# Reordering one period of attention A, a double-buffered last attention B and compact keys in a two-attention, two-feed-forward kernel

## The chip, the cores and the metric

The kernel runs on one core of a Trainium2 chip. The metric is the device time of one execution in microseconds (us). Engines are named as in the profile: PE (TensorE), with PEld for its weight loads, DVE (VectorE), ACT (ScalarE), POOL (GpSimd) and SP (SyncE, here only a queue that issues DMAs).

## The reference

Input x has 8 batches of 512 tokens with 256 features; all is float32. Four residual layers follow each other, each behind a layer norm:

```python
x = x + attn_a(norm(x))
x = x + ffn(norm(x))
x = x + attn_b(norm(x))
x = x + ffn(norm(x))
```

```python
# attn_a: 16 heads of 64; per token and head, a 64 x 64 causal table of q_i * k_j
scores = einsum('bshq,bshk->bshqk', Q / 8, K), masked above the diagonal
attn = einsum('bshqk,bshk->bshq', softmax(scores), V) @ Wo + bo
# attn_b: usual causal attention over 512 tokens, 16 heads of 16
y = softmax(q @ k.T / 4, causal) @ v;  y @ W_proj + b_proj
# ffn: hidden 1024, ternary weights with a scale per row
h = silu(x @ w1) * (x @ w2);  h = gelu(h @ h1);  h = gelu(h @ h2);  h @ w3
```

Attention A is unusual: no token looks at another. Each token and head has a table of products q_i * k_j, its exponential, and two sums over j, with weights 1 and v_j. It is element-wise work for DVE, POOL and ACT, not for PE.

## The kernel before

**Two streams.** The first stream is attention A (class AttentionA). Its unit is a *period*: one batch b, one of NG = 4 groups of 4 heads and one of NT = 4 tiles of 128 tokens, 128 periods in all. The second stream (after_a) is the rest: feed-forward 1, attention B and feed-forward 2 of each batch. It runs one batch behind A and shares the engines with it. The last batch's second stream has no attention A beside it.

**Order.** The kernel is recorded with a manual schedule: instructions stand on each engine in the order in which the Python calls them, and each engine works in that order. `step(n)` writes one of four steps of a period, in three parts, so a period has twelve *slots*. After each part the second stream is drawn on, generator by generator, until the cost it has announced with `yield` has reached its share of `total` = 301.7 per 16 periods. Small steps of the second stream (scales, layer norm, copies, products of hi and low halves) are put off with `later` and called at the next `flush`.

**A period.** The causal table of 64 x 64 is cut into squares off the diagonal. There are four units: u = 0 and 2 are the 32-squares of two heads each (tile `w`, 128 x 4096, three buffers), u = 1 the 16-squares of four heads (`w16`, one buffer), u = 3 the squares of 8, 4, 2 and 1 (`ws`). For a unit:

- `scores` (L796): products q * k, on POOL for u = 0 and 2 and on DVE for 1 and 3. For u = 0 also the diagonal, `acc` (L783).
- `exps` (L810, with L805 for the diagonal): exponential on ACT.
- `weigh` (L820, L817): times v on DVE.
- `halve` (L826): a DMA issued from POOL adds the upper half of the tile to the lower one (not for `ws`).
- `fold` (L831): POOL adds halves once more, for the 32-squares.
- `gather` (L857): DVE reduces what is left to sums per row, `red`.
- `add_rows` (L864): POOL adds the sums into `acc`; `small_squares` (L847, L864) does so for the squares of 2 and 1.

Then `invert` (L868, DVE), `divide` (L872, POOL), `turn_group` (L880, PE transposes), the copy `att` (L730, ACT), `project_out` (L888, L483, PE) and `new_x` (L899, ACT). Ahead of a period stand `project` (L753 for k, L758 for q and v, PE), which also has SP load the next group's weights, and `keep_qk` (L773 and L774, ACT copies of k and q). For the first group of a batch, `normalise`, the transposes `turn_x` (L559) and their copy come earlier still.

**PSUM.** Of eight banks two hold `qv`, five rotate in `ps_f` for the second stream, and one, `bank`, is cut into two halves of 256 columns for k, the transposed x, the transposed result and its projection. `half_bank()` gives the halves in turn.

**Second stream.** `Normed` normalises a tile: `moments` on DVE (L535, L536), `scales` on POOL (L540 to L543), `normed` on ACT (L549, L553), transposes on PE (L559), a copy on ACT (L988), for the feed-forward its low part on DVE (L995). The feed-forward multiplies in two halves, hi and low: gates L1064, `silu` L1040 (ACT), L1043 (DVE), L1047 (ACT) and L1048 (POOL); hidden layers L1126 (PE), L1097 and L1098 (ACT), L1102 (DVE); the last product L1159. Weights are loaded by DMAs issued from POOL (L946). Attention B: projections `pqkb` L1205 with copies L1226, values `pvb` L1243, and for 4 groups of four heads and 4 key blocks `scores` (L1260, mask L1264, exponential L1267) and `values` (L1272).

Of the kernel before, what the change touches and what calls it, by code (L numbers as in the profile page):

```python
# [9 lines left out]
F32 = mybir.dt.float32  # L10
# [25 lines left out]
BG = BH * SLOT // P  # L36

FH = 1024
MC = FH // P
HB = 2048  # L40

# [243 lines left out]
def fast_path(ctx: ExitStack, tc: tile.TileContext, k, t, flag):  # L285
# [154 lines left out]
    wbqk_d = dram.tile([P, HB], F32, name="wbqk_d")  # L440
# [5 lines left out]
    def later_weights():  # L446
# [7 lines left out]
        wbqk = block("wbqk").rearrange("p (c f) -> p c f", c=DC)  # L454
        rows = block("rows")
        wbvp = block("wbvp")[:, : 2 * DC * D].rearrange("p (j c f) -> p j c f", j=2, c=DC)
        n_qk = 2 * BG * P
        nc.sync.dma_start(wbqk, t.w_bqkb.rearrange("(c p) j f -> p c (j f)", p=P))
        nc.sync.dma_start(wbvp[:, 0], t.w_bvb.rearrange("(c p) f -> p c f", p=P))
        nc.sync.dma_start(wbvp[:, 1], t.w_bp.rearrange("(c p) f -> p c f", p=P))  # L460
        nc.sync.dma_start(rows[0:1, :n_qk], t.w_bqk[D - 1 : D].rearrange("o j f -> o (j f)"))
        nc.sync.dma_start(rows[0:1, n_qk : n_qk + D], t.w_bv[D - 1 : D])
        yield
        for w, off, width in ((wbqk, 0, 2 * GW), (wbqk, 2 * GW, 2 * GW), (wbvp[:, 0], 0, D)):
            row = rows[0:1, n_qk if width == D else off :][:, :width]
            pss = [less_row(w[:, c, off : off + width], c, row, 0) for c in range(DC)]
            yield
            for c, ps in enumerate(pss):
                nc.scalar.copy(w[:, c, off : off + width], ps)
            yield  # L470
# [20 lines left out]
    turn = [0]  # L491


    bank = ps_a.tile([P, 2, GW], F32, name="bank")
    halves = [0]

    def half_bank():
        halves[0] ^= 1
        return bank[:, halves[0], :]
# [78 lines left out]
    def pieces(w, n, off, nsq, cols):  # L578

# [7 lines left out]
        if n < 16:  # L590
            e, ev = (
                w[:, a * SMALL + off : a * SMALL + off + nsq * n * n].rearrange("p (x i j) -> p x i j", i=n, j=n)
                for a in range(2)
            )
            yield e, ev, lambda v: of_rows(v).unsqueeze(3), lambda v: of_cols(v).unsqueeze(2)
            return
        both = w.rearrange("p (b a x i j) -> p a b x i j", a=2, x=nsq, i=n, j=JB)
        if n == 32:
# [7 lines left out]
        else:  # L606
            for k in range(n // JB):
# [5 lines left out]
                )  # L613

    class AttentionA:
# [3 lines left out]
        def __init__(self):  # L619
# [5 lines left out]
            self.ready, self.sums = set(), []  # L625
            self.todo = [
                (b, i, g, u) for b in range(NB) for g in range(NG) for i in range(NT) for u in range(NU)
            ]
            self.steps = len(self.todo) + 11
# [16 lines left out]
        def at(self, n):  # L646
            return self.todo[n] if 0 <= n < len(self.todo) else (None,) * 4

        def step(self, n):

            weighed = self.at(n - 2)
            if weighed[0] is not None:
                self.weigh(*weighed)
            unit = self.at(n)
            on_pool = unit[3] in (0, 2)
            if on_pool:
                half = self.scores(*unit)
                next(half)
            if weighed[0] is not None:
                self.halve(*weighed)  # L660
            if on_pool:
                next(half, None)
            b, i, g, u = self.at(n + 40)
            if u == 0 and g == 0 and i == 0 and b > 0:
                self.x[b] = load_x(b)
            b, i, g, u = self.at(n + 10)
            if u == 0 and g == 0 and i == 0 and b > 0:
                self.measure(b)
            b, i, g, u = self.at(n + 8)
            if u == 0 and g == 0:  # L670
                self.live["xn"] = normed(self.x[b][:, i, :], *self.rn[b, i], "a")
            b, i, g, u = self.at(n - 5)
            if u == NU - 1:
                self.invert(b, i, g)
            b, i, g, u = self.at(n - 4)
            if u == 1:
                self.gather(b, i, g, u)
            b, i, g, u = self.at(n + 7)
            if u == 0 and g == 0:
                nc.scalar.copy(self.live[b, i], self.live.pop("ps_ln"))  # L680
            if self.at(n - 1)[0] is not None:
                self.exps(*self.at(n - 1))
            yield
            if unit[0] is not None and not on_pool:
                for _ in self.scores(*unit):
                    pass
            for args in self.sums:
                self.add_rows(*args)
            self.sums = []
            b, i, g, u = self.at(n - 5)  # L690
            if u == NU - 1:
                self.divide(b, i, g)
            b, i, g, u = self.at(n - 2)
            if u == NU - 1:
                self.small_squares(b, i, g)

            b, i, g, u = self.at(n - 4)
            if u == 0:
                self.fold(b, i, g, u)
            b, i, g, u = self.at(n - 3)  # L700
            if u == 2:
                self.fold(b, i, g, u)
            b, i, g, u = self.at(n - 9)
            if u == NU - 1:
                self.new_x(b, i, g)
            b, i, g, u = self.at(n + 2)
            if u == 0:
                self.keep_qk(b, i, g)
            b, i, g, u = self.at(n - 7)
            if u == NU - 1:  # L710
                self.turn_group(b, i, g)
            b, i, g, u = self.at(n - 8)
            if u == NU - 1:
                self.project_out(b, i, g)
            b, i, g, u = self.at(n + 3)
            if u == 0:
                self.project(b, i, g)
            yield
            b, i, g, u = self.at(n - 4)
            if u == 2:  # L720
                self.gather(b, i, g, u)
            b, i, g, u = self.at(n - 5)
            if u == 0:
                self.gather(b, i, g, u)
            b, i, g, u = self.at(n - 3)
            if u == NU - 1:
                self.gather(b, i, g, u)
            b, i, g, u = self.at(n - 7)
            if u == NU - 1:
                nc.scalar.copy(self.live["att"], self.live.pop("pta"))  # L730
            b, i, g, u = self.at(n + 8)
            if u == 0 and g == 0:
                self.live[b, i] = lnp.tile([P, DC, P], F32, tag="xnt_a", name=f"xnta_{b}_{i}", bufs=NT)
                self.live["ps_ln"] = turned_over(self.live.pop("xn"), half_bank().rearrange("p (c s) -> p c s", c=DC))
            yield
# [11 lines left out]
        def project(self, b, i, g):  # L747
# [3 lines left out]
            pk = half_bank()  # L751
# [17 lines left out]
        def keep_qk(self, b, i, g):  # L769
# [3 lines left out]
            nc.scalar.copy(kt[:, 0], pk)  # L773
            nc.scalar.copy(kt[:, 1], qv[:, 0])  # L774
            self.live[b, i, g] = [qv, kt]

        def scores(self, b, i, g, n_u):

            qv, kt = self.live[b, i, g][:2]
            if n_u == 0:  # L780
                acc = ap_.tile([P, 2, GW], F32, tag="acc", name=f"acc_{b}_{i}_{g}", bufs=3)
                self.live[b, i, g].append(acc)
                nc.vector.tensor_tensor(acc[:, 0, :], qv[:, 0], kt[:, 0], ALU.mult)  # L783

            if n_u in (0, 2):
                w = wt.tile([P, 4096], F32, tag="w", name=f"w_{b}_{i}_{g}_{n_u}", bufs=3)
            elif n_u == 1:
                w = wt.tile([P, 4096], F32, tag="w16", name=f"w16_{b}_{i}_{g}")
            else:
# [702 lines left out]
```

## Time and profile before

| what | us |
|---|---|
| median of three executions | 3910.99 (3909.09 to 3912.19) |
| the profiled execution, its own time | 3906.43 |
| span of the profiled execution | 3904.6 |
| PE busy | 2962.9 (76%) |
| DVE busy | 3462.5 (89%) |
| ACT busy | 2459.7 (63%) |
| POOL busy | 3081.7 (79%), without the DMA issues |

The costliest groups of instructions, from the page (line, engine, operation, out<-in, count, busy us and mean ns of one, idle time of the engine before them and its releaser):

```profile
L796 POOL TENSOR_TENSOR w<-k 128x1024 f32<-128x1024 f32 x512 | 1077.1, 2104 | 7.5 <-ACT k L774 6.9
L820 DVE TENSOR_TENSOR w<-w,qv 128x1024 f32<-128x1024 f32 x768 | 898.6, 1211 | 9.9 <-ACT w L810 9.9
L831 POOL TENSOR_TENSOR w<-w 128x1024 f32<-128x1024 f32 x256 | 642.6, 2510 | 45.3 <-DMA w<-w 44.9
L826 POOL DMA_DIRECT2D w<-w x384 | 338.9, 883 | 326.2 <-issue 138.4
```

The span falls into a start, a long stretch in which both streams run (from about 480 to 3580 us, some 450 us for each batch), and the last batch's second stream alone (from about 3580 us). An idle time in these lists counts only if the engine is the one that sets the pace there.

### The profile page before, as it was taken

How to read it: one execution, taken by the hardware profiler on the slowest of the kernel's cores; microseconds unless marked ns; L12 is line 12 of the kernel's file. 1: busy time of each engine (PE TensorE's matmuls, PEld its weight loads, DVE VectorE, ACT ScalarE, POOL GpSimd, SP SyncE). 2: the span in 40 equal slices, each digit the busy share in tenths (PEclk: the TensorE clock that was granted, in tenths of full speed). 3: DMA queues.
4: the chain of work that ended last, by engine and by line, in shares of the span. 5: the costliest groups of instructions: out<-in, count | busy, mean ns of one | idle time of the engine just before them, and what ended most of it. 6: DMA issues, size and time to landing. Idle time of an engine off the chain costs nothing.

```text
span 3904.6 us, 37527 instructions
## 1 busy us (share of the span) xinstructions
PE 2962.9 (76%) x12080; PEld 1981.4 (51%) x12080; DVE 3462.5 (89%) x3906; ACT 2459.7 (63%) x3332; POOL 3081.7 (79%) x3052
## 2 busy tenths in 40 slices
PE   5653487687876977778876878778876878778988
PEld 2331264365634655356643656346653556346747
DVE  7999999998999999999999999999989999997216
ACT  3443476577765876667765877667765777655443
POOL 6888888888788888888888888888888888886211
PEclk6556598888987989888997989879898899879999
DMA  8766677678875877768876778768776678666305
GB/s 225 172 137 141 152 194 164 143 176 202 210 156 128 207 196 184 153 157 215 208 166 130 191 195 203 158 140 217 182 191 144 164 192 220 152 137 200 130 25 187
DMA packets 117306, 668.04 MB, mean 171 GB/s; under 512 B 12774, under 2 KB 30825, under 8 KB 42603
## 3 DMA queue, kind: packets, MB, share of 16 engines
q0 software_dynamic: 80640, 587.24, 65.4%
q1 hardware_dynamic: 36460, 78.31, 5.8%
q8 instruction: 98, 1.61, 0.2%
q14 instruction: 108, 0.88, 0.1%
HBM read 253.94 MB, written 8.91 MB: 67 GB/s over the span
## 4 chain that ended last, share of the span: by engine, by line
DVE 43%; PE 17%; POOL 15%; ACT 9%; DMA 8%; issue 8%; SPq 0%; POOLq 0%; DVEq 0%; ACTq 0%
DVE red L857 16%; DVE w L820 11%; DMA w<-w 8%; PE ph L1126 7%; POOL w L796 4%; DVE ws L796 4%; DVE ws L820 3%; ACT w L810 3%; POOL w L831 3%; POOL acc L864 2%; DVE w L796 2%; PE pw L1064 2%; PE pqkb L1205 2%; DVE acc L868 2%; POOL h L1048 2%
## 5 line engine op out<-in xcount | busy, mean ns | idle before, releaser
L1126 PE MATMUL ph<-h,hidden 128*128 128x512 f32 x4096 | 1047.7, 413 | 71.1 <-POOL h L1048 48.7
L796 POOL TENSOR_TENSOR w<-k 128x1024 f32<-128x1024 f32 x512 | 1077.1, 2104 | 7.5 <-ACT k L774 6.9
L810 ACT ACTIVATE w<-w 128x2048 f32<-128x2048 f32 x384 | 734.2, 1912 | 480.8 <-POOL w L796 380.3
L1126 PEld LDWEIGHTS ph<-h,hidden 128*128 128x128 f32 x4096 | 796.0, 196 | 270.5 <-POOL h L1048 57.8
L820 DVE TENSOR_TENSOR w<-w,qv 128x1024 f32<-128x1024 f32 x768 | 898.6, 1211 | 9.9 <-ACT w L810 9.9
L831 POOL TENSOR_TENSOR w<-w 128x1024 f32<-128x1024 f32 x256 | 642.6, 2510 | 45.3 <-DMA w<-w 44.9
L857 DVE TENSOR_REDUCE red<-w 128x128 f32<-128x1024 f32 (+1 forms) x384 | 601.0, 1565 | 65.9 <-POOL w L831 38.3
L826 POOL DMA_DIRECT2D w<-w x384 | 338.9, 883 | 326.2 <-issue 138.4
L864 POOL TENSOR_TENSOR acc<-acc,red 128x256 f32<-128x256 f32 (+1 forms) x640 | 471.2, 736 | 120.0 <-DVE red L857 99.7
L857 DVE TENSOR_REDUCE red<-ws 128x256 f32<-128x2048 f32 (+1 forms) x256 | 435.3, 1741 | 0.0
L758 PE MATMUL qv<-wqv,xnta 128*128 128x512 f32 x512 | 300.4, 717 | 94.4 <-DVE ws L820 78.9
L810 ACT ACTIVATE ws<-ws 128x1920 f32<-128x1920 f32 x128 | 231.5, 1809 | 143.5 <-DVE ws L796 142.9
L1064 PE MATMUL pw<-xnt,gate 128*128 128x512 f32 (+2 forms) x1152 | 308.4, 429 | 14.1 <-ACT silu L1040 5.3
L796 DVE TENSOR_TENSOR w<-qv,k 128x1024 f32<-128x1024 f32 x256 | 301.1, 1218 | 3.7
L796 DVE TENSOR_TENSOR ws<-qv,k 128x1024 f32<-128x1024 f32 (+3 forms) x512 | 299.4, 645 | 0.0
L820 DVE TENSOR_TENSOR ws<-ws,qv 128x1024 f32<-128x1024 f32 (+3 forms) x512 | 295.6, 638 | 3.5 <-ACT ws L810 3.3
L1064 PEld LDWEIGHTS pw<-xnt,gate 128*128 128x128 f32 x1152 | 239.8, 222 | 70.3 <-ACT silu L1040 8.7
L1267 ACT ACTIVATE eb<-psb 128x256 f32<-128x256 f32 (+3 forms) x512 | 181.9, 443 | 129.0 <-PE psb L1264 128.6
L1102 DVE TENSOR_TENSOR h<-ph,h 128x512 fp32r<-128x512 f32 x256 | 169.0, 682 | 97.1 <-ACT ph L1098 91.2
L880 PE MATMUL bank<-ident,acc 128*128 128x128 f32 x256 | 61.1, 327 | 255.4 <-ACT k L773 253.9
L1097 ACT ACTIVATE h<-ph,s_sb 128x512 fp32r<-128x512 f32 x256 | 176.5, 690 | 108.1 <-PE ph L1126 106.0
L753 PE MATMUL bank<-wk,xnta 128*128 128x256 f32 x512 | 166.5, 456 | 99.8 <-ACT x L899 94.8
(153 smaller groups left out, 5042.2 us busy)
## 6 DMA issues: line engine op xcount, KB each, us to landing
w<-w POOLq DMA_DIRECT2D x384, 1024.0 KB, 7.7
hidden<-in_h POOLq DMA_DIRECT2D x128, 1024.0 KB, 7.7
gate<-in_w12p POOLq DMA_DIRECT2D x32, 1024.0 KB, 9.2
w<-in_w3p POOLq DMA_DIRECT2D x16, 1024.0 KB, 5.3
wqv<-wqv_d SPq DMA_DIRECT2D x31, 512.0 KB, 4.6
wo<-in_wo SPq DMA_DIRECT2D x32, 256.0 KB, 6.0
wbqk<-wbqk_d SPq DMA_DIRECT2D x8, 1024.0 KB, 6.8
w<-in_h SPq DMA_DIRECT2D x8, 1024.0 KB, 6.4
```

Source lines behind the costliest of these rows:

```text
L758: nc.tensor.matmul(qv.rearrange("p j f -> p (j f)"), xnt[:, c, :], wqv[:, c, :], start=(c == 0), stop=(c == DC - 1),)
L796: eng.tensor_tensor(e, rows(q).to_broadcast(shape), columns(kt[:, 0]).to_broadcast(shape), ALU.mult)
L810: nc.scalar.activation(e, e, AF.Exp, scale=C**-0.5)
L820: nc.vector.tensor_tensor(ev, e, columns(qv[:, 1]).to_broadcast(list(e.shape)), ALU.mult)
L826: nc.gpsimd.dma_start(w[:, :2048], w[:, 2048:], accum_op=ALU.add)
L831: nc.gpsimd.tensor_tensor(w[:, :1024], w[:, :1024], w[:, 1024:2048], ALU.add)
L857: nc.vector.tensor_reduce(red, self.columns_of(w, n, off, nsq), AX.X, ALU.add)
L864: nc.gpsimd.tensor_tensor(rows, rows, part.rearrange("p a (x i) -> p a x i", i=n), ALU.add)
L1064: nc.tensor.matmul(pj[:, toks], w[:, m % 4, j, c, :], xs[:, p, c, toks], start=(p == 0 and c == 0), stop=(p == 1 and c == DC - 1),)
L1097: nc.scalar.activation(h(0, m), pj, AF.Gelu, scale=scale)
L1126: nc.tensor.matmul(pss[j], w[:, j, c, :], h_in(p, c), start=(p == 0 and c == 0), stop=(p == 1 and c == MC - 1),)
L1267: nc.scalar.activation(es[h], scs[h], AF.Exp)
```

## The change

**The order of a period** is no longer written in `step`, but in a table G["order"] of (slot, action, arguments). `slot(t)` calls for each entry the action of the period n with t = 12 n + slot; actions of one slot come in the order of the table. A period reaches from slot -120 to slot 40.

| action | slot before | slot after |
|---|---|---|
| normalise, turn_x, its copy | -24, -22, -21 | -25, -22, -20 |
| project, keep_qk | -8, -5 | -6, -2 |
| scores u = 0, 1, 2, 3 | 0, 4, 6, 10 | 0 and 1, 4, 6, 10 |
| exps u = 0, 1, 2, 3 | 3, 6, 9, 12 | 3, 6, 9, 12 |
| weigh u = 0, 1, 2, 3 | 6, 9, 12, 15 | 5, 9, 12, 13 |
| halve u = 0, 1, 2 | 6, 9, 12 | 6, 9, 12 |
| fold u = 0, 2 | 13, 16 | 13, 17 |
| small_squares | 16 | 14 |
| gather u = 1, 0, 3, 2 | 15, 17, 20, 20 | 15, 16, 19, 21 |
| adds u = 1, 0, 3, 2 | 16, 19, 22, 22 | 20, 20, 21, 22 |
| invert, divide | 24, 25 | 24, 25 |
| turn_group, copy att | 31, 32 | 28, 32 |
| project_out, new_x | 34, 37 | 33, 40 |

Within a period DVE then does, from the reciprocal on: first product of the next period, `ws` weighing, `w16` reduce, first `w32` reduce, `w16` products, diagonal and first `w32` weighing, reduces of 8 and 4, `w16` weighing, second `w32` reduce, `ws` products, second `w32` weighing. Before, the first `w32` reduce stood behind the `w16` products, the second ahead of the reduces of 8 and 4, and the first product ahead of the reciprocal. POOL: the sums of `w16` and of the squares of 8 and 4 are now added ahead of the `w16` halving, which in turn stands ahead of the last add; before, the `w16` sums were added between the first fold and the small squares.

**PSUM halves.** `half_bank()` is gone; each use has a fixed half: k and the transposed x take half 0, the transposed result and its projection half 1.

**Pace.** The second stream is drawn on after each slot, with the same delay as before and `total` = 298.1.

**Attention B.** Keys are packed 16 columns a head (2 groups of 128 instead of 4); queries keep 32 columns a head, with zeros beside the 16 of the head, and heads are taken in an order that puts two of one key slot into neighbouring groups. Score matmuls keep their number and size; the key projection has two groups fewer. In the last batch (`alone`) the scores take seven PSUM banks in turn (four of `ps_f`, two of `qv`, and `bank`), the exponentials two blocks in turn, and a step's scores stand ahead of the previous step's values.

Other branches that the table opens (sums by transposes on PE, a split of `w16` with POOL, a gelu remainder on PE) are not taken with these values: `sum` is dve, `p16` is 0, `gelu`, `lo`, `div` and `first` are not set.

```diff
+G = {'sum': ['dve', 'dve'], 'p16': 0, 'rot': 3, 'half': [0, 0, 1, 1, 0, 1],
+ 'order': [[12, 'weigh', 2], [40, 'new_x'], [6, 'scores', 2, 0, 2], [9, 'exps', 2], [12, 'exps', 3],
+           [24, 'invert'], [-25, 'normalise'], [6, 'halve', 0], [32, 'keep_att'], [21, 'adds', 3],
+           [3, 'exps', 0], [33, 'project_out'], [0, 'scores', 0, 0, 2], [1, 'scores', 0, 1, 2],
+           [25, 'divide'], [20, 'add32', 0], [12, 'halve', 2], [-120, 'load'], [22, 'add32', 2],
+           [-20, 'keep_x'], [20, 'adds', 1], [6, 'scores', 2, 1, 2], [-30, 'ahead'], [5, 'weigh', 0],
+           [-22, 'turn_x'], [14, 'small_squares'], [-2, 'keep_qk'], [-6, 'project'], [15, 'gather', 1],
+           [10, 'scores', 3, 0, 1], [17, 'fold', 2], [9, 'weigh', 1], [9, 'halve', 1], [6, 'exps', 1],
+           [16, 'sums32', 0], [4, 'scores', 1, 0, 1], [28, 'turn_group'], [19, 'gather', 3], [13, 'fold', 0],
+           [21, 'sums32', 2], [13, 'weigh', 3]]}
...
-    def half_bank():
-        halves[0] ^= 1
-        return bank[:, halves[0], :]
+    def bank_half(j):
+        return bank[:, j, :]
...
+        def slot(self, t):
+            now = []
+            for lo, hi, order in TABLES:
+                for place, (slot, what, args) in enumerate(order):
+                    n, r = divmod(t - slot, 12)
+                    if r == 0 and lo <= n < hi:
+                        now.append((place / len(order), what, self.todo[n] + args))
+            for _, what, args in sorted(now, key=lambda p: p[0]):
+                getattr(self, what)(*args)
...
-        for j in range(2):
-            pps = [None] * BG
+        for j, groups in enumerate((BG, KG)):
+            pps = [None] * groups
...
+        alone = b == NB - 1
+        exps = [block(f"eb_{b}_{n}").rearrange("p (h q) -> p h q", q=S) for n in range(1 + alone)]
...
+        def score_bank(name):
+            n, taken[0] = taken[0] % 7, taken[0] + 1
+            if not alone or n < 4:
+                return ps_f.tile([P, S], F32, tag="pf", name=name)
+            if n < 6:
+                return ps_qv.tile([P, S], F32, tag="qv", name=name)
+            return bank.rearrange("p j f -> p (j f)")
...
-                    scs[h], qk[1][slots[h], g, keys], qk[0][slots[h], g, j * P :], start=True, stop=False
+                    scs[h], qk[1][slots[h], g // 2, keys], qk[0][slots[h], g, j * P :], start=True, stop=False
...
-                if before is not None:
+                if before is not None and not alone:
                     values(*before)
                 es = scores(g, j)
+                if before is not None and alone:
+                    values(*before)
...
-        for n in range(-10, a.steps):
-            for part, _ in enumerate(a.step(n)):
-                if n >= 3 and part == 2:
-                    next(prep, None)
-                while 3 * spent * each < total * (3 * (n - each - 11) + part + 1):
-                    spent += next(done)
+        for at in a.slots:
+            a.slot(at)
+            if at >= 9 and at % 3 == 2:
+                next(prep, None)
+            while spent * 12 * NT * NG < total * (at + 1 - 12 * NT * NG - 33):
+                spent += next(done)
```

## The prediction

> **What bounds the kernel now.** I read the page first (busy shares, slices, chain), then a table of stretches, then the idle time of VectorE and GpSimd by line inside the long stretch, then two timelines.
>
> ```profile
> DVE  7999999998999999999999999999989999997216
> POOL 6888888888788888888888888888888888886211
> DVE 43%; PE 17%; POOL 15%; ACT 9%; DMA 8%; issue 8%; SPq 0%; POOLq 0%; DVEq 0%; ACTq 0%
> ```
>
> VectorE (DVE) is nearly full for 37 of 40 slices with GpSimd (POOL) close behind, and DVE leads the chain. The last three slices are a tail of another kind. The stretches show both (columns: length, busy PE, PEld, DVE, ACT, POOL, clock, DMA share, GB/s):
>
> ```profile
> 480.00:3580.00 3100.00, 2422.51 (x10181) 1643.63 (x10182) 2903.49 (x3289) 2136.48 (x2871) 2630.51 (x2591) 0.88 0.75 177
> 3580.00:3904.60 324.60, 293.73 (x1405) 213.88 (x1404) 110.69 (x140) 128.85 (x251) 58.86 (x96) 0.96 0.35 124
> 2115.30:2181.60 66.30, 49.34 (x181) 35.65 (x181) 59.71 (x83) 42.28 (x58) 56.38 (x64) 0.80 0.63 145
> 2066.60:2090.36 23.76, 16.22 (x97) 7.40 (x96) 23.73 (x25) 14.77 (x28) 20.71 (x19) 0.79 0.66 133
> ```
>
> A period without feed-forward work (the last line) leaves DVE 0.03 us idle: there a new order gains nothing. Over the long stretch DVE is idle 3100 - 2903.5 = 196.5 us, two gate periods (third line) holding 6.6 of it. In the tail TensorE (PE) is busy 90% and sets the end. What ends DVE's idle time in the long stretch, then the same for two rows of POOL:
>
> ```profile
> L857 DVE TENSOR_REDUCE red<-w 128x256 f32<-128x2048 f32 x329 | 515.3, 1566 | 51.5 <-POOL w L831 31.2 <-DMA w<-w 19.2
> L1043 DVE SCALAR_TENSOR_TENSOR silu<-pw,s_sb,silu 128x512 f32<-128x512 f32 x112 | 82.8, 739 | 51.5 <-ACT silu L1040 51.3
> L995 DVE TENSOR_TENSOR xnt<-ps_ln,xnt 128x256 fp32r<-128x256 f32 x56 | 22.4, 413 | 38.9 <-ACT xnt L988 38.9
> L1102 DVE TENSOR_TENSOR h<-ph,h 128x512 fp32r<-128x512 f32 x216 | 141.8, 681 | 26.0 <-ACT ph L1098 25.8
> L864 POOL TENSOR_TENSOR acc<-acc,red 128x256 f32<-128x256 f32 (+1 forms) x549 | 403.9, 736 | 108.4 <-DVE red L857 90.9
> L880 PE MATMUL bank<-ident,acc 128*128 128x128 f32 x218 | 50.0, 316 | 208.7 <-ACT k L773 207.1 <-POOL w L831 1.4
> ```
>
> Only 51.5 us of DVE's idle time belongs to attention A's own reductions; 116 us are feed-forward steps whose code and pace stay.
>
> **The Trainium skill.** "Perfetto Trace Analysis", Identifying Performance Opportunities: take the most occupied engine, find its gaps, and treat regimes apart; this trace has those two regimes. "DMA: Bandwidth & Descriptors", SWDGE vs HWDGE vs iDMA: accumulating DMAs go through GpSimd only; here the halving DMAs hold POOL 0.88 us each, so moving them moves POOL. "TensorE: Matmul & The Clock Gate", Part 3: four K=32 matmuls side by side reach 3.07x and M=32 columns behave alike. The trace agrees for K=32: 8 score matmuls take 1.07 us to the next row, alone 8 x 0.43 = 3.44 (0.43 is the spacing of the 128x512 pqkb loads), 3.2x.
>
> **The change, part by part.**
>
> (1) The last batch's attention B. One group of heads in the tail, ACT then PE:
>
> ```profile
> 3751.73 2.07 ACT L1267 ACTIVATE eb<-psb 128x512 f32<-128x512 f32 x4 [0.71 <-PE psb L1264]
> 3756.01 1.64 ACT L1267 ACTIVATE eb<-psb 128x384 f32<-128x384 f32 x4 [2.21 <-PE psb L1264]
> 3750.33 1.14 PE L1260 MATMUL psb<-qkb,qkb 32*128 32x512 f32 x8
> 3752.38 2.51 PE L1272 MATMUL pyb<-eb,vb 128*32 128x512 f32 x8 [0.58 <-ACT eb L1267]
> 3763.18 1.14 PE L1260 MATMUL psb<-qkb,qkb 32*128 32x512 f32 x8
> ```
>
> PE and ACT take turns: 3763.18 - 3750.33 = 12.85 us a group. With seven score banks, two exponential blocks and the next scores put ahead of the values, they overlap. ACT needs 2.07 + 1.64 + 1.21 + 0.79 + 0.59 (copy) = 6.3. PE needs scores 1.07 + 0.86 + 0.65 + 0.43 = 3.0, masks 4 x 0.33 = 1.3, and values, seen only while they wait for ACT: at most 6.5 as now, at least 2.8 (the skill's 3.07x on 3.44, times 1280/512 columns). I take 2.8: PE 7.1, ACT 6.3, with hand-over 7.5. Gain 4 x (12.85 - 7.5) = 21; with values at 6.5, 4 x (12.85 - 10.8) = 8.
>
> (2) Compact keys: two projection groups fewer, each 4 x 0.43 = 1.7 us of PE and one ACT copy (0.6). In the tail PE carries the end: -3.4. In the seven other batches PE has room (22% idle): 0. The pace total falls by the same 2 x 1.8, so both streams stay in step: 0. Tail: -24.8 (from -11 to -27).
>
> (3) DVE's order. Counts and durations per period do not change. The w32_0 reduce moves ahead of the two w16 products (2.35 us earlier), the w32_2 reduce ahead of the small-square products, the first product behind the reciprocal. Does the earlier reduce find its data? In the plain period the reciprocal starts at 2066.64, POOL's halving issue at 2067.13, and the fold ends at 2070.34 + 2.64 = 2072.98, that is 5.85 after the issue. In the new order the issue is due just after the reciprocal's start, so the fold ends at about +5.95; the reduce comes at reciprocal 1.66 + product 0.33 + small squares 2.2 + w16 reduce 2.3 = +6.5. Half a microsecond in hand, where 2.3 more were: 0 taken, up to +25 (0.2 us in each period) if POOL is late there.
>
> (4) POOL's order. The add of the w16 sums leaves the place behind the first fold, where POOL stood for DVE's reduce (most of the 90.9 us), and the adds of the 8- and 4-squares go ahead of the w16 halving, where POOL waited 2.74 us in the plain period. DMA landing is 7.7 us, so a halving issued earlier lands earlier. What lies behind the stands is the second fold, half the scores and the halvings: the 51.5 us. Taken: half, -25 (bounds 0 and -51). The silu wait ends on ACT, itself behind POOL's h L1048; less standing on POOL gives a fifth: -10 (0 to -25). The xnt chain runs through POOL's small scale steps: -3 (+10 to -15). h L1102 waits for ACT's own speed: 0 (+-10).
>
> (5) PSUM halves, later key copy. L880 waits 207 us for the key copy of the other half: the wait is between halves, so fixing them removes little; turn_group comes three slots earlier and will wait for the x copy instead. qv L758's 48.7 us go: the projection is two slots later and the last weighing two earlier. PE has room, so 0 (+10 to -10). The projection takes its two weight loads on SP along; they land in 4.6 us and are wanted a period later: 0. keep_qk moves from slot -5 to -2, behind the third exponential. Queued behind it on ACT is the ws exponential; DVE's first product and POOL's next scores wait for it. It ends 1.91 + 0.76 = 2.7 us after the second score half; POOL has 0.7 + 3 x 0.75 + 0.9 + 0.7 = 4.5 of other work there, so 1.8 us remain: 0, but a gelu group on ACT (4.0 us with its table load) between the two takes it.
>
> Sum: tail -24.8, long stretch -38: -63 on the execution's own 3906.4 (span 3904.6 plus 1.8) gives 3843.6; the median shown is 4.6 higher, so 3848.
>
> **Rivals.** The bound of no change is 0.2%, 8 us.
> A, forecast, 0.55: 3848, own range 3815 to 3882.
> B, 0.18: the long stretch keeps its idle time because it belongs to the feed-forward steps; for it the 116 us, against it the 51.5. 3911 - 25 = 3886 (to 3902 with slow values).
> C, 0.12: POOL's stands were the root of most gaps, silu and xnt too; half of 196 goes: 3911 - 25 - 98 = 3788, or 3749 at 70%. For it: POOL at 56.4 busy plus some 6 of issues in the 66.3 us gate stretch.
> D, 0.11: slower. The key copy, behind the third exponential and now also behind project_out in the shared bank, comes late; DVE and POOL both stand. It decides from (25 + 8) / 112 periods = 0.3 us a period; a gelu group ahead of it in half the periods, 2.2 us beyond the 1.8 of slack, one half absorbed, is 112 x 0.5 x 1.1 = 62: 3911 + 62 - 25 = 3948. Against it: k was ready early before (in the plain period it ends at 2078.3, the product starts at 2090.0) and three slots are some 6 us.
> E, 0.04: the layout costs what the tail gains, no measurable change; so too if the layout does nothing and the overlap fails.
>
> Chances: faster 0.85, same 0.04, slower 0.11. Range 3780 to 3908: A, B and part of C, leaving about 2 in 10 outside.
>
> **What would show it.** Right: a group of heads in the tail takes 7 to 8 us; DVE idle before the reduces falls to about 25; POOL's wait on red falls under 40; plain periods stay at 23.7. Wrong: the key copy as releaser of DVE acc or POOL w with several us in total (D); idle before the w32_0 reduce grown (3); silu and xnt waits unchanged and the reduces' too (B).

## The result, and the profile after

| what | us |
|---|---|
| median of the changed kernel | 3867.19 (3857.84 to 3870.38) |
| median of the kernel before, beside it | 3911.59 (3909.09 to 3916.82) |
| ratio | 0.9881, 95% interval 0.9859 to 0.9902 |
| the profiled execution of the changed kernel | 3870.38, span 3868.6 |

Faster by 44 us, or 1.2%; 3848 was forecast, 19 us less, and the range held the time. The profiled execution is the slowest of the four; its span is 36 us shorter than that of the kernel before.

The changed kernel has other line numbers: products L801, weighing L836, halving L843, fold L851, reduces L984, adds L998; `project` L749 for k and L754 for q and v, the key copy L771; `turn_group` L1020, its copy `att` L1024, `new_x` (from here on the x copy) L1045; attention B's `pqkb` L1362 with its copies L1383. A plain period is one without feed-forward work beside it. The changed kernel's page, rows of busy tenths and the chain's shares:

```profile
DVE  7999999999999999999999989999989899898216
POOL 6888888888888888888888888888888878788211
DVE 41%; PE 24%; POOL 15%; ACT 7%; issue 7%; DMA 6%; POOLq 0%; SPq 0%; ACTq 0%; DVEq 0%
```

DVE still leads. Its line now has five 8s, all from the 24th slice on, where before there were two, one of them early: some of the gain is lost again in the later batches. At the last reciprocal of a batch's attention A the changed kernel is ahead by 24 us in the fourth batch and by 11 in the seventh. The table of stretches (length, busy PE, PEld, DVE, ACT, POOL, clock, DMA share, GB/s): the long stretch, then one plain period from reciprocal to reciprocal, then the tail.

```profile
480.00:3560.00 3080.00, 2388.43 (x10085) 1639.06 (x10084) 2874.75 (x3272) 2111.86 (x2834) 2626.16 (x2573) 0.87 0.75 176
...
1125.73:1149.33 23.60, 14.13 (x79) 6.48 (x80) 23.60 (x26) 12.90 (x25) 20.97 (x18) 0.78 0.76 164
3560.00:3868.60 308.60, 285.79 (x1428) 215.54 (x1426) 119.40 (x151) 132.23 (x259) 66.39 (x104) 0.95 0.39 138
```

Over the long stretch DVE is idle 3080 - 2874.75 = 205 us, no less than the 196.5 before. The stretch is nevertheless shorter, because DVE has less to do in it: between the 16th and the last reciprocal its busy time falls from 2954.6 to 2938.6 us, most of it since a period takes some 0.12 us less of DVE (the plain one 23.60 instead of 23.72). From the last reciprocal of attention A to the end there are 292.5 us instead of 315.8; the last reciprocal comes 12.8 us earlier. What ends DVE's idle time in the long stretch (busy and mean; idle and releasers), then the same for POOL, PE and ACT:

```profile
L836 DVE TENSOR_TENSOR w<-w,qv 128x1024 f32<-128x1024 f32 x655 | 767.4, 1213 | 48.0 <-ACT w L824 48.0
L984 DVE TENSOR_REDUCE red<-w 128x256 f32<-128x2048 f32 x327 | 506.5, 1568 | 45.4 <-POOL w L851 33.2 <-DMA w<-w 12.0
L1190 DVE SCALAR_TENSOR_TENSOR silu<-pw,s_sb,silu 128x512 f32<-128x512 f32 x112 | 82.5, 745 | 26.8 <-ACT silu L1187 26.8
L1142 DVE TENSOR_TENSOR xnt<-ps_ln,xnt 128x256 fp32r<-128x256 f32 x52 | 20.7, 420 | 30.5 <-ACT xnt L1135 30.5
```

```profile
L998 POOL TENSOR_TENSOR acc<-acc,red 128x256 f32<-128x256 f32 (+1 forms) x545 | 388.1, 712 | 22.1
L801 POOL TENSOR_TENSOR w<-k 128x1024 f32<-128x1024 f32 x435 | 930.4, 2139 | 87.2 <-ACT k L771 86.7
L1020 PE MATMUL bank<-ident,acc 128*128 128x128 f32 x218 | 59.1, 365 | 341.3 <-ACT x L1045 243.2 <-ACT xnta L728 88.6 <-POOL w L851 4.1
L1024 ACT COPY att<-bank 128x256 f32<-128x256 f32 x109 | 41.1, 377 | 31.8 <-PE bank L749 31.8
```

The reduces wait 45 us (51.5 before), silu 27 (51.5), POOL's adds 22 (108). New are 48 us at DVE's weighing behind ACT's exponential (10 in the whole execution before) and 87 us of POOL's products behind the key copy (7 before). PE's transposes wait 243 us for the x copy; before, they waited 207 us for the key copy instead. The tail on PE, one group of heads from its first scores (L1429, 128x512) to the next group's:

```profile
3729.80 1.14 PE L1429 MATMUL psb<-qkb,qkb 32*128 32x512 f32 x8
...
3733.01 1.35 PE L1441 MATMUL pyb<-eb,vb 128*32 128x512 f32 x8
...
3737.43 0.70 PE L1429 MATMUL psb<-qkb,qkb 32*128 32x512 f32 x2
...
3740.95 1.06 PE L1441 MATMUL pyb<-eb,vb 128*32 128x512 f32 x8 [0.23 <-ACT eb L1436]
...
3745.07 0.69 PE L1429 MATMUL bank<-qkb,qkb 32*128 32x512 f32 x1
```

3745.07 - 3737.43 = 7.64 us a group, and 7.63 for the one before it, instead of 12.85. Eight value matmuls of 512 columns take 2.37, 1.35, 1.06 and 1.34 us in the four groups, where they took 2.42 to 2.51 with waits for ACT.

### The profile page after: what moved, and what is told of

It is laid out like the page before. It is cut to its first block, busy times and chain, and to the rows that moved or that the text cites. A ratio compares the mean times of both kernels' runs of the same rounds, so it can differ in the third digit from the quotient of the medians.

```text
span 3868.6 us, 37899 instructions
## 1 busy us (share of the span) xinstructions
PE 2865.3 (74%) x12016; PEld 1963.0 (51%) x12016; DVE 3440.7 (89%) x3906; ACT 2441.4 (63%) x3310; POOL 3092.5 (80%) x3052
## 4 chain that ended last, share of the span: by engine, by line
DVE 41%; PE 24%; POOL 15%; ACT 7%; issue 7%; DMA 6%; POOLq 0%; SPq 0%; ACTq 0%; DVEq 0%
DVE red L984 13%; DVE w L836 12%; PE ph L1283 11%; DMA w<-w 5%; DVE w L801 4%; POOL w L801 4%; DVE ws L801 4%; DVE ws L836 3%; POOL h L1195 2%; DVE acc L1004 2%; PE pqkb L1362 2%; POOL acc L998 2%; ACT w L824 2%; PE qv L754 2%; PE pot L1316 2%
## 5 line engine op out<-in xcount | busy, mean ns | idle before, releaser
L801 POOL TENSOR_TENSOR w<-k 128x1024 f32<-128x1024 f32 x512 | 1096.1, 2141 | 95.4 <-ACT k L771 94.9
L1283 PE MATMUL ph<-h,hidden 128*128 128x512 f32 x4096 | 1068.3, 419 | 43.2 <-POOL h L1195 35.2
L836 DVE TENSOR_TENSOR w<-w,qv 128x1024 f32<-128x1024 f32 x768 | 899.4, 1212 | 52.1 <-ACT w L824 52.1
L1283 PEld LDWEIGHTS ph<-h,hidden 128*128 128x128 f32 x4096 | 811.3, 200 | 248.3 <-POOL h L1195 45.7
L851 POOL TENSOR_TENSOR w<-w 128x1024 f32<-128x1024 f32 x256 | 645.9, 2523 | 81.1 <-DMA w<-w 80.4
L984 DVE TENSOR_REDUCE red<-w 128x128 f32<-128x1024 f32 (+1 forms) x384 | 594.2, 1567 | 55.2 <-POOL w L851 33.2
L843 POOL DMA_DIRECT2D w<-w x384 | 342.7, 892 | 268.9 <-DVE w L836 198.6
L1020 PE MATMUL bank<-ident,acc 128*128 128x128 f32 x256 | 71.1, 372 | 550.2 <-ACT x L1045 395.3
L998 POOL TENSOR_TENSOR acc<-acc,red 128x256 f32<-128x256 f32 (+1 forms) x640 | 455.9, 712 | 26.6
L984 DVE TENSOR_REDUCE red<-ws 128x256 f32<-128x2048 f32 (+1 forms) x256 | 435.5, 1742 | 0.0
L1020 PEld LDWEIGHTS bank<-ident,acc 128*128 128x128 f32 x256 | 33.6, 178 | 594.2 <-issue 358.4
L836 DVE TENSOR_TENSOR ws<-ws,qv 128x1024 f32<-128x1024 f32 (+3 forms) x512 | 298.8, 645 | 6.1 <-ACT ws L824 5.8
L801 DVE TENSOR_TENSOR w<-qv,k 128x1024 f32<-128x1024 f32 x256 | 300.2, 1214 | 0.0
L801 DVE TENSOR_TENSOR ws<-qv,k 128x1024 f32<-128x1024 f32 (+3 forms) x512 | 299.4, 647 | 0.0
L754 PE MATMUL qv<-wqv,xnta 128*128 128x512 f32 x512 | 275.4, 665 | 0.0
L1436 ACT ACTIVATE eb<-psb 128x512 f32<-128x512 f32 (+3 forms) x503 | 180.2, 446 | 111.5 <-PE psb L1433 110.0
```

The costliest lines, as they stand in the source:

```text
L754: nc.tensor.matmul(qv.rearrange("p j f -> p (j f)"), xnt[:, c, :], wqv[:, c, :], start=(c == 0), stop=(c == DC - 1),)
L801: eng.tensor_tensor(e, rows(q).to_broadcast(shape), columns(kt[:, 0]).to_broadcast(shape), ALU.mult)
L836: nc.vector.tensor_tensor(ev, e, columns(qv[:, 1]).to_broadcast(list(e.shape)), ALU.mult)
L843: nc.gpsimd.dma_start(w[:, :2048], w[:, 2048:], accum_op=ALU.add)
L851: nc.gpsimd.tensor_tensor(w[:, :1024], w[:, :1024], w[:, 1024:2048], ALU.add)
L984: nc.vector.tensor_reduce(red, self.columns_of(w, n, off, nsq), AX.X, ALU.add)
```

## The experiments

| kernel | median us | ratio to the kernel before, 95% interval |
|---|---|---|
| the changed kernel | 3867.2 | 0.9881 (0.9859 to 0.9902) |
| e1_no_overlap | 3883.0 | 0.9921 (0.9907 to 0.9934) |
| e2_old_table | 3921.0 | 1.0024 (1.0015 to 1.0033) |
| e3_x_copy_37 | 3824.0 | 0.9776 (0.9762 to 0.9789) |
| e4_early_k | 3912.7 | 0.9997 (0.9989 to 1.0005) |
| e5_reduce_back | 3925.5 | 1.0028 (1.0019 to 1.0038) |
| e6_add16_back | 3874.4 | 0.9898 (0.9883 to 0.9913) |
| e7_turn_31 | 3825.2 | 0.9774 (0.9761 to 0.9787) |
| e8_old_halves | 3921.1 | 1.0015 (1.0009 to 1.0022) |
| e9_old_pace | 3886.1 | 0.9935 (0.9920 to 0.9949) |
| e10_new_pace | 3858.8 | 0.9862 (0.9846 to 0.9877) |
| e11_37_31 | 3820.5 | 0.9757 (0.9741 to 0.9772) |
| e12_37_31_pace | 3818.1 | 0.9767 (0.9754 to 0.9781) |

Each series had the kernel before beside it, with medians from 3910.7 to 3914.7. All of these kernels compute the same function with the same instructions; they differ in places and waits. Lines of their profiles below are from 480 to 3540 us; in that window the changed kernel's lines have the idle times above, but for a few tenths, PE's L1020 apart (337.1).

**The overlap alone, undone.**

```diff
-        alone = b == NB - 1
+        alone = False
```

> The changed kernel with the last batch's attention B written as in all other batches (one exponential block, only the rotating banks, values ahead of the next scores). Theory (step 1 of the prediction): the overlap alone gave 4 x (12.85 - 7.63) = 21 us in the tail; the time goes from 3867 to 3888 (3883 to 3893), the tail behind the last reciprocal from 292.5 to 313.5, and a group of heads takes some 12.8 us again. Rival: the shorter groups come from somewhere else, such as the compact keys or the fixed bank halves; then the tail stays within 5 us and the time at 3867 to 3872.

3883.0, 16 us more. On the trace a group of heads takes 12.86 us again, and the stretch of attention B's exponentials in the tail, from the first start to the last end, goes from 29.3 back to 49.6 us. The tail is 309.4 us, 17 more; A's last reciprocal came 6 us earlier in this profile, although nothing ahead of it was touched. The theory holds: the overlap is worth 16 to 20 us.

**The whole order, undone.** The table takes the slots of before and, within a slot, the order of before.

```diff
- [16, 'sums32', 0], [21, 'sums32', 2], [5, 'weigh', 0], [13, 'weigh', 3], [20, 'adds', 1]
+ [17, 'sums32', 0], [20, 'sums32', 2], [6, 'weigh', 0], [15, 'weigh', 3], [16, 'adds', 1]
...
- [-2, 'keep_qk'], [-6, 'project'], [28, 'turn_group'], [33, 'project_out'], [40, 'new_x']
+ [-5, 'keep_qk'], [-8, 'project'], [31, 'turn_group'], [34, 'project_out'], [37, 'new_x']
```

> The changed kernel with the slots and the order of before written into the table; the fixed bank halves, the pace total of 298.1, the overlap of the last attention B and the compact keys stay. Theory: of the 44 us gained, the tail holds 23 and the new order of the period the rest; the time is 3882 to 3890, plain periods take 23.7 us again, the add of sums on POOL waits about 100 us for red again. Rival: the order is worth nothing and the gain ahead of the tail comes from the fixed halves and compact keys: 3867 (3861 to 3873).

3921.0: the order is worth 54 us here, far more than the 15 to 23 expected. With its shorter tail this kernel ought to be 25 us faster than the kernel before, and is slower. Something beside the order cost it some 35 us. Three candidates were left: the compact keys themselves, the fixed halves and the second stream's new pace.

**Fixed halves.** The old table again, the halves taken in turn as before the change.

```diff
     def bank_half(j):
-        return bank[:, j, :]
+        halves[0] ^= 1
+        return bank[:, halves[0], :]
```

> The old order in the new table (3921 us, 8 above the kernel before although its tail is 29 us shorter) with the two halves of the PSUM bank taken in turn again, as before the change; the pace total of 298.1 stays. Theory: the fixed halves cost the old order some 37 us ahead of the tail; with the halves in turn the time is 3880 to 3890. Rival: halves of one bank wait for each other in either way, and what the old order loses comes from the second stream's new pace; then 3915 to 3925.

3921.1 against 3921.0: the halves are worth nothing in this order. The Trainium skill, "PSUM — Partial Sum Buffer", section "PSUM bank collisions raise a hardware error", tells a program to guard PSUM by bank and 32-partition quadrant, not by address, and that would explain it. The profile agrees: ACT's copy `att`, from half 1, waits 31.8 us for the key projection L749 into half 0 (line above). Whichever half is used, then, a projection, its copy, the next transposes and their copy stand in one chain.

**The pace.** The old table, and the two key groups left out still counted:

```diff
                 yield 1.8 if j > 0 else 0.6
+            for g in range(groups, BG):
+                yield 1.8
...
-    total = G.get("total", 298.1)
+    total = G.get("total", 301.7)
```

> The old order in the new table, and the second stream paced as before the change: the two key groups that compact keys leave out are still counted at 1.8 each, and the total is 301.7. VectorE and GpSimd then have the order of the kernel before to the last instruction; what remains of the change is compact keys, fixed halves and the overlap of the last attention B. Theory: the new total puts second-stream work up to two slots later beside attention A, and that alone cost the old order some 38 us ahead of the tail (3921 against 3913 - 25); with the old pace the time is 3880 to 3890. Rival: compact keys themselves or the fixed halves cost it; then the time stays at 3915 to 3925.

> The changed kernel with only this same old pace (1.8 counted for each key group left out, total 301.7). Theory: the pace is worth as much in the new order as in the old, the time falls by 30 to 40 us to 3827 to 3837, most of it in the periods in which attention B starts. Rival: what the pace costs depends on where the order puts the waits of TensorE; in the new order the waits for the x copy stay, and the time changes by less than 12 us either way (3855 to 3879).

e9 gives 3886.1. DVE and POOL have the order of the kernel before to the last instruction, and what is left of the change brings 25 us (ratio 0.9935). So the new pace alone, the total with what is announced, cost the old order 35 us, and the compact keys cost nothing ahead of the tail. In the new order the medians differ by only 8 us (e10, 3858.8), which is not clear of the noise, since the intervals overlap; the rival's "less than 12" holds, the theory's 30 does not. In e10 the period in which attention B starts is 33 us shorter over the seven batches, but the others together are about as much longer. The two old-order kernels at DVE's weighing, the new pace (e2) first:

```profile
L836 DVE TENSOR_TENSOR w<-w,qv 128x1024 f32<-128x1024 f32 x641 | 750.8, 1213 | 26.5 <-ACT w L824 26.5
```

```profile
L836 DVE TENSOR_TENSOR w<-w,qv 128x1024 f32<-128x1024 f32 x650 | 761.2, 1212 | 2.4 <-ACT w L824 2.3
```

From reciprocal to reciprocal, the period in which attention B starts is longer by 22 us over the seven batches in e2, and one in the hidden layers of feed-forward 2 by 15. Within one period ACT waits for PE's `pqkb` and has the exponential behind it, first e2, then e9 at the same place:

```profile
1099.46 1.09 ACT L1383 ACTIVATE qkb<-pqkb 128x512 f32<-128x512 f32 x2 [5.99 <-PE pqkb L1362]
```

```profile
1095.31 2.07 ACT L1383 ACTIVATE qkb<-pqkb 128x512 f32<-128x512 f32 x4 [3.29 <-PE pqkb L1362]
```

That the pace is the cause is shown; that it works through these copies is what the traces suggest.

**VectorE's reduce.** One entry goes back behind the two w16 products.

```diff
- [16, 'sums32', 0], [4, 'scores', 1, 0, 1]
+ [4, 'scores', 1, 0, 1], [17, 'sums32', 0]
```

> The changed kernel with only VectorE's reduce of the first w32 tile moved back behind the two w16 products (slot 17). Theory (step 3 of the prediction in the light of the traces): the earlier reduce saves 0.11 us a period, since the product no longer overwrites the tile just reduced (+14 us without it), and loses some 19 us where the fold is late, above all in the third period of each batch; undone, the plain period is 23.7 us again, the third period some 2.5 us shorter, the time 3858 to 3868. Rival: the early reduce is a loss outright, as GpSimd is late in most periods with feed-forward work, and the time falls to 3840 to 3855.

3925.5: 58 us lost, more than the whole gain of the change, and neither theory nor rival had the sign. DVE's own waits for the fold indeed go. Of the 58 us some 13 may be a later start of the product behind the reduce (0.12 us, 111 times, see the last section). POOL's groups say what else came:

```profile
L801 POOL TENSOR_TENSOR w<-k 128x1024 f32<-128x1024 f32 x428 | 920.1, 2150 | 191.2 <-DVE red L984 141.9 <-ACT k L771 49.1
```

Even in a plain period POOL stands, as the timeline of POOL in e5 shows:

```profile
2087.00 2.37 POOL L851 TENSOR_TENSOR w<-w 128x1024 f32<-128x1024 f32 x1 [0.50 <-DMA w<-w]
2090.62 1.96 POOL L801 TENSOR_TENSOR w<-k 128x1024 f32<-128x1024 f32 x1 [1.24 <-DVE red L984]
2092.52 0.86 POOL L843 DMA_DIRECT2D w<-w  x1
```

`w` has three buffers. The reduce of the first 32-squares is the last reader of one of them, and POOL's products for u = 2 of the next period write into it. Its end therefore sets when POOL may start, and with POOL what stands behind it there. On DVE this does not show at attention A's waits (the reduces wait 29 us in all instead of 45, the weighing 46 instead of 48) but at the feed-forward's: silu waits 35 us instead of 27, layer norm's second moment step 26 instead of 16, and the hidden layers, first in the changed kernel, then in e5:

```profile
L1249 DVE TENSOR_TENSOR h<-ph,h 128x512 fp32r<-128x512 f32 x208 | 134.7, 683 | 17.2 <-ACT ph L1245 17.2
```

```profile
L1249 DVE TENSOR_TENSOR h<-ph,h 128x512 fp32r<-128x512 f32 x208 | 135.9, 683 | 42.3 <-ACT ph L1245 42.3
```

The early reduce was priced by whether it finds its data; its worth lies in whom it lets go. The Trainium skill, "Perfetto Trace Analysis", section "Identifying Performance Opportunities", says that a gap that repeats on the engine that should be saturated can mean too few buffers for the next tile; the 142 us on POOL, the second busiest engine, look like such a gap. No run gave `w` a fourth buffer, so that the loss comes by way of the buffer is read from the traces. In the kernel before, the same stand was probably booked elsewhere: POOL waited for the reduce at its adds.

**POOL's adds.** The sums of w16 and the small squares go back between the folds.

```diff
- [20, 'adds', 1]
+ [16, 'adds', 1]
...
- [14, 'small_squares']
+ [16, 'small_squares']
```

> The changed kernel with the add of the w16 sums and the small squares moved back to slot 16 on GpSimd, between the two folds. Theory (step 4): GpSimd stands for VectorE's reduce again (22 us of it now, about 100 before), the second fold and the next scores come later, and VectorE's waits for the fold and for the silu copies grow by as much as the move was held to bring: the time rises by 20 to 35 us, to 3887 to 3902. Rival: GpSimd's stands are filled from its slack, 3867 (3861 to 3873).

```profile
L998 POOL TENSOR_TENSOR acc<-acc,red 128x256 f32<-128x256 f32 (+1 forms) x541 | 393.2, 727 | 100.6 <-DVE red L984 87.6
```

POOL stands 100.6 us at its adds, 87.6 of them for the reduce, as before, and the median rises by 7 us (3874.4), which is not clear of the noise, not by 20 to 35. POOL's stands at the adds were slack in the main: silu waits 40 us again instead of 27, but the weighing and the hidden layers wait some 5 and 3 us less.

**TensorE's wait for the x copy.** One entry each:

```diff
- [40, 'new_x']
+ [37, 'new_x']
```

```diff
- [28, 'turn_group']
+ [31, 'turn_group']
```

> The changed kernel with only new_x moved from slot 40 back to 37. Theory: TensorE's transposes of the next result waited 243 us for this copy, the work of attention B behind them ran late, ACT's copies waited for it and with them the exponentials and DVE; with the copy earlier that wait falls under 60 us, VectorE's wait for the exponential of w at its weighing falls from 48 to about 25, and the time is 3840 to 3855. Rival: TensorE has room, the wait is only where its idle time shows, and its place is taken by another: 3867 (3861 to 3873).

> The changed kernel with only the transposes of the result (turn_group) moved from slot 28 back to 31; the copy new_x stays at 40. Moving new_x three slots earlier took 43 us off. Theory: what counts is the distance on TensorE between the x copy that frees the bank and the next transposes, because the second stream's matmuls and with them ScalarE stand behind that wait; three slots of distance from the other side do the same, the 243 us of waiting for the x copy fall under 100 and the time is 3825 to 3845. Rival 1: it was the earlier copy on ScalarE itself that helped; then nothing is gained here, 3861 to 3873. Rival 2: the transposes, now one slot ahead of their own copy, make ScalarE wait for TensorE, and a loss of 10 us or more follows.

> The changed kernel with new_x at slot 37 and turn_group at 31 together (alone they gave 3824 and 3825). Theory: both remove the same wait of TensorE, so together they give little more: 3815 to 3825, VectorE left with waits of some 50 us for the fold and the halving, 30 for xnt and 27 for silu. Rival: the 115 us that TensorE still waits for the x copy ahead of the next projection, with turn_group at 31 alone, are worth as much again: below 3805.

Slots 28 and 40 both fall on the fifth of a period's twelve slots, so the transposes stand right behind the x copy of the period before; either edit puts three slots between them. 3824.0, 3825.2 and both together 3820.5: some 45 us, from either side, and not twice; the first is more than the theory gave it. That it works from the side of the transposes, with the copy where it was, rules out that the copy's place on ACT was the point. How the wait reaches DVE is seen where attention B starts; the changed kernel's timelines of PE, ACT and DVE:

```profile
2892.09 0.66 PE L1020 MATMUL bank<-ident,acc 128*128 128x128 f32 x2 [3.27 <-ACT x L1045]
2892.54 6.32 PE L1362 MATMUL pqkb<-xnt_b,wbqk 128*128 128x512 f32 x8
```

```profile
2888.80 1.91 ACT L824 ACTIVATE w<-w 128x2048 f32<-128x2048 f32 x1
2890.60 1.08 ACT L1383 ACTIVATE qkb<-pqkb 128x512 f32<-128x512 f32 x2
2891.55 0.39 ACT L1045 COPY x<-bank 128x256 f32<-128x256 f32 x1
2896.20 0.60 ACT L1383 ACTIVATE qkb<-pqkb 128x512 f32<-128x512 f32 x1 [4.25 <-PE pqkb L1362]
2898.90 0.60 ACT L1383 ACTIVATE qkb<-pqkb 128x512 f32<-128x512 f32 x1 [2.10 <-PE pqkb L1362]
2899.39 1.90 ACT L824 ACTIVATE w<-w 128x2048 f32<-128x2048 f32 x1
```

```profile
2901.33 2.35 DVE L836 TENSOR_TENSOR w<-w,qv 128x1024 f32<-128x1024 f32 x2 [4.91 <-ACT w L824]
```

PE stands 3.27 us for a copy that itself stands behind an exponential and two other copies; the projections `pqkb` behind the transposes come late; ACT stands 4.25 and 2.10 us for them with the next exponential behind it; DVE stands 4.91. This period takes 33.9 us. With the copy three slots earlier the same place has no wait on PE, and the period takes 26.8 (e3, PE then DVE):

```profile
2858.95 0.38 PE L1020 MATMUL bank<-ident,acc 128*128 128x128 f32 x2
```

```profile
2866.63 2.35 DVE L836 TENSOR_TENSOR w<-w,qv 128x1024 f32<-128x1024 f32 x2
```

Over the seven batches the periods in which attention B starts were 39 us longer in the changed kernel than in the kernel before; they are 30 us shorter again in e3 and in e7. DVE's weighing waits 14 us in all where it waited 48 (e3):

```profile
L836 DVE TENSOR_TENSOR w<-w,qv 128x1024 f32<-128x1024 f32 x654 | 766.2, 1213 | 14.3 <-ACT w L824 14.3
```

The length of PE's wait is not the measure: in e3 L1020 still waits 187 us, for other releasers; in e7 the wait, 158 us, stands at the projection L749; in e11 14 us are left there. All three come out alike.

**The key copy.**

```diff
- [-2, 'keep_qk'], [-6, 'project']
+ [-5, 'keep_qk'], [-8, 'project']
```

> The changed kernel with project and keep_qk moved from slots -6 and -2 back to -8 and -5. Theory: GpSimd's first scores waited 87 us for the key copy; that wait falls under 15, the fold and the halvings behind it come earlier, and the time falls by 5 to 15 us, to 3852 to 3862. Rival: GpSimd is not the bound where it waits, and the time stays at 3867 (3861 to 3873) with its idle time moved to another line; a projection two slots earlier waits for the qv banks (34 to 49 us of it before), which could cost a few us.

3912.7, 45 us slower. POOL's and PE's groups in e4:

```profile
L801 POOL TENSOR_TENSOR w<-k 128x1024 f32<-128x1024 f32 x429 | 922.9, 2151 | 0.1
```

```profile
L749 PE MATMUL bank<-wk,xnta 128*128 128x256 f32 x428 | 175.9, 552 | 332.0 <-ACT x L1045 237.2 <-ACT xnta L728 94.8
```

POOL's wait for k is gone to the last tenth, and the time is that of the kernel before. PE's wait for the x copy now stands ahead of the projection, so eight projection matmuls instead of two transposes come between that wait and the second stream. Most of the loss lies in two periods with feed-forward work, 16 and 15 us over the seven batches. In one of them ACT stands 3.97 us for the gates behind the projection:

```profile
1257.18 0.69 ACT L1187 ACTIVATE silu<-pw,s_sb 128x512 f32<-128x512 f32 x1 [3.97 <-PE pw L1211]
```

This is what the traces suggest; the edit moves the projection and the copy together, and which of the two costs more stays open.

**Everything that helped.** new_x 37, turn_group 31 and the old pace:

> new_x at slot 37, turn_group at 31 and the old pace (1.8 counted for each key group left out, total 301.7) together: 3820 without the pace. Theory: the pace was worth 8 us because it changed which matmuls of the second stream stood behind TensorE's wait for the x copy; without that wait it is worth nothing, 3814 to 3826. Rival: the two add up, 3808 to 3814 or below.

3818.1, no different from 3820.5: without PE's stand behind the x copy the pace is worth nothing. Both are faster than either kernel of the change, by 47 and 49 us than the changed one. What is left on DVE there are 50 to 62 us at the reduces, 30 at xnt and 21 to 27 at silu.

## Why the prediction was near, point by point

| step | forecast | measured |
|---|---|---|
| (1) overlap | -21 | -16 (e1); the exponentials' stretch -20.3 |
| (2) compact keys, tail | -3.4 | the stretch of `pqkb` in the tail, first to last start, 15.5 to 12.4, -3.1 |
| (1) and (2), with the order of before (e9) | -24.8 | -25 |
| (3), (4) and (5), all slots, at the old pace (e9 to e10) | -38 | -27 |
| (2) pace of the second stream (e10 to the changed kernel) | 0 | +8, not clear of noise |
| sum | -63 | -44 |

The sum came near in part by luck: one step taken at 0 was worth 58 us, another taken at 0 cost 43.

**(1) and (2), the tail,** were right term by term. The doubtful price, the values, came near its lower end in three groups of four: 1.06 to 1.35 us for eight matmuls where 2.8 x 512/1280 = 1.12 was taken, 2.37 in the first. A group takes 7.64 us where 7.5 was taken.

**(2), "both streams stay in step: 0"** was wrong. Taking the same 3.6 from the cost and from the total keeps them in step only at a batch's end; in between the second stream is drawn later ahead of the key projections and earlier behind them, with 2.3 slots between the two (3.6/298.1 of a batch's 192). That cost 35 us in the old order; the 8 here are within the noise.

**(3), DVE's order, taken at 0,** failed as a step. It asked whether the earlier reduce finds its data (it does, but for 33 us of waiting for the fold, 31 before) and not who waits for the reduce. Taken back alone, it costs 58 us. Some 13 of these may belong to a second miss: the time on DVE did change, by 0.12 us in nearly every period.

**(4), POOL's order, taken at -38,** had the size near and the cause wrong. The stand behind the adds did fall under 40, but it was slack in the main (e6: 7 us, within the noise); the reduces' wait did not halve. What the term was to bring came, by e5 and e6, with the early reduce of (3). silu did gain: 25 us less waiting, where 10 were taken, and e6 gives 13 of them back.

**(5), PSUM and the key copy, taken at 0,** holds a loss of more than the 19 us that are missing. "Will wait for the x copy instead" was seen; "PE has room, so 0" is the step that failed. PE has room on average, but it works in order, and behind this wait stood what ACT waited for with the exponentials behind it. Three slots of distance more are worth 42 to 43 us. The slack of 1.8 us for the key copy did not hold either, POOL waits 87 us for it; but e4 and e11 (12 us of that wait, 47 us gained) show that this was a symptom more than a price. No run takes all the slots of (5) back together: back alone, the earlier projection and key copy cost 45 us and the x copy or the transposes gain 43, so what (5) costs as a whole stays open.

Rival D named the key copy as the mechanism of a loss. Its lines are in the trace and it did not decide. Rival C, POOL's stands as the root of most gaps, fails for the stands at the adds (e6) and holds in part for those at the products (e5). Rival B, gains in the tail alone, is ruled out by e9 against the changed kernel, with intervals that don't meet.

## What to carry to other kernels

When a reader is moved, ask not only whether its data is there but who waits for its end, if only for the buffer: here the place of one reduce was worth 58 us, more than any other single move. A wait on an engine with room is free only if nothing behind it feeds an in-order engine that has the bound's work in its queue; follow PE to ACT to DVE before writing a 0. And when work is dropped from a paced stream, keep its pace first and change it in a run of its own.

## What the hardware showed unexpectedly

DVE started a product later when it overwrote the tile just reduced. In the kernel before, the `w16` reduce started at 2070.50 and the product into `w16` at 2072.81, 2.31 us later; the second reduce took 1.13 to its next. After, both reduces together take 2072.21 to 2075.53 = 3.32, that is 2.19 + 1.13. It is so throughout the kernel before: 107 times this product comes next and starts after 2.30 to 2.32 us, and the profile names the reduce as what it waited for; 21 times an instruction comes next that doesn't write `w16`, after 2.19 to 2.20. With e5's order the plain period is 23.7 again. It is so in e4 too, with the new order, but there the second reduce stands for POOL's fold. No run changed the tile alone.

Eight value matmuls side by side (128x512, 32 columns each) took 1.06 us in the best of four groups and 1.34 to 1.35 in two more: 3.2 and 2.6 times faster than eight of the 0.43 us pqkb matmuls in a row (3.44). In the first group they took 2.37. The Trainium skill, "TensorE: Matmul & The Clock Gate", Part 3, gives 2.38 for three such tiles and 3.07 for four tiles of rows; the measured 2.6 to 3.2 for four tiles of columns fit with that. Why the first group is slower was not looked into.
